# Two-layer graph attention on one core: the projections as seven half-size products, statistics moved ahead, normalization on ScalarE

## The chip, the cores and the metric

One core of a Trainium2 chip runs the whole program. The metric is device time in microseconds, the median of three runs. A core has five engines that run beside each other and wait for one another by semaphores: TensorE (PE, matmuls; its weight loads are shown as PEld), VectorE (DVE), ScalarE (ACT), GpSimd (POOL) and SyncE (SP), which only issues transfers. Each engine takes its own instructions in the order in which the program wrote them.

## What is computed

Two layers over 4096 nodes with 512 features, both with the same 4096 x 4096 matrix `adj`. Cut to what matters:

```python
h = relu(layernorm(x))
q, k, v = h @ Wq.T + bq, h @ Wk.T + bk, h @ Wv.T + bv
x = x + softmax(q @ k.T / sqrt(512) + 2 * adj) @ v          # layer 0
h = relu(layernorm(x))
nX = normalize_per_head(h @ W)                               # 8 heads of 64
att = softmax(where(adj != 0, leaky_relu(at1 + at2.T) * adj, -32768))
x = x + elu(att @ nX + nX)                                   # layer 1
```

## The kernel before, in words

The kernel has three stages, one after the other. The projections (0 to 271 us of the profile) make everything that layer 0 needs of `x`; then comes attention of layer 0, to about 2100 us, in which the features of layer 1 are also made; then attention of layer 1. The change lies in the first stage only.

The projections go by eight blocks (`sb`, 0 to 7) of 512 rows each. A block is four tiles of 128 rows. What is done with a block:

- `load_x` (L531) fetches its rows on SP's queue into `xt`, which has two buffers.
- `normalize` (L537) subtracts the mean and multiplies by the inverse root of the variance. The statistics are `means` (L167; eight DVE instructions, L172 and L173). The root is `inverse_root` (L156): a power on GpSimd (L159), then four small instructions (L161 to L164) on the engine that the caller names, here DVE. Then DVE normalizes the four tiles (L543).
- `hidden` (L548) turns the rows on PE (16 transposes, L553) into `pt`, which has two PSUM buffers; ACT applies the relu and writes `hT` (L554). GpSimd makes four sums and differences of half-size parts of `hT`, called `hS` (L562 to L565). Both are stored, for attention needs them again: it computes the scores by seven half-size products in the form of Strassen's algorithm.
- `values_of` (L570) multiplies `hT` by Wv: 16 matmuls of 128x512 (L574) into `pv`, four PSUM buffers, each read once by DVE, which adds the bias (L578).
- `queries` (L583) multiplies by one matrix A. Since q and k are only used as q times k, Wq and Wk are multiplied once at the start into A (`a_sb`; L648, copied by ACT at L652), and the biases go into the vector `c_sb` (L653). These are again 16 matmuls of 128x512 (L588) into `pq`, the same four PSUM buffers; DVE adds `c_sb`, scales and writes the columns in another order into `qs` (L592). `qs` is stored (L596); GpSimd makes four half-size differences `ts` of it (L605 to L608), stored as well (L610).

The order is written out by hand: `seq` keeps every instruction where the program put it on its engine's queue. After a start, in which the weights are loaded and A is made, round `sb` (1 to 7) is: normalize block sb+1, load block sb+2, values of sb, hidden of sb+1, queries of sb. Some work for layer 1 is slipped in ahead of `queries`: in round 2 `center_weights` (three DVE instructions, L230 to L232), in rounds 3 to 6 `weigh_weights` (L234), which twice lets GpSimd multiply (L237) and DVE sum the product (L238).

At the start come, in this order: block 0 normalized and turned; Wq and Wk transposed on DVE as they land (L464); values of block 0; block 1 normalized; `attention_vectors` (L192; small DVE work for layer 1 and four transfers on ACT's queue); A; `c_sb`; hidden of block 1; queries of block 0.

Lines of later stages that are used below as measures: L719 is a 128x256 matmul of attention in layer 0, L727 the DVE add that reads such a result from PSUM; L258 to L262 are the mean and root of layer 1's normalization, on GpSimd, and L268 is its normalization on ACT.

Of the kernel before, what the change touches and what calls it, by code (L numbers as in the profile page):

```python
# [10 lines left out]
F32 = mybir.dt.float32  # L11
BF16 = mybir.dt.bfloat16
AF = mybir.ActivationFunctionType
ALU = mybir.AluOpType
# [4 lines left out]
P = 128  # L19
# [59 lines left out]
def fast_path(  # L79
# [29 lines left out]
    def sources_of_rows(t):  # L109

        return t.rearrange("p (q c r) -> p c q r", c=SB, r=R)
# [336 lines left out]
    with tc.tile_pool(name="early", bufs=2) as early, tc.tile_pool(name="kv", bufs=1) as kv:  # L448
# [14 lines left out]
        def turn_blocks(t, raw, c):  # L463
            seq(nc.vector.transpose(t.rearrange("p (m r) -> p m r", r=R), raw[:, :, ts(c, R)]))  # L464
# [53 lines left out]
        with tc.tile_pool(name="proj_c", bufs=1) as pc, tc.tile_pool(  # L518
# [10 lines left out]
            bv_sb = early.tile([P, D], F32, name="bv_sb", tag="qt", bufs=16)  # L529

            def load_x(sb):  # L531
                xt = early.tile([P, SB, D], F32, name="xt", tag="ag", bufs=2)
# [1 line left out]
                    seq(nc.sync.dma_start(out=xt[:, b, :], in_=x[ts(sb * SB + b, P), :]))  # L534
                return xt

            def normalize(xt):  # L537
                mv = means(work, [xt[:, b, :] for b in range(SB)], "h")
                var = work.tile([P, SB], F32, name="hv", tag="hv", bufs=1)
                seq(nc.vector.tensor_scalar_add(var, mv[:, :, 1], LN_EPS))  # L540
                rstd = inverse_root(nc.vector, work, var, SB, "h")
                for b in range(SB):
                    seq(nc.vector.tensor_scalar(  # L543
                        xt[:, b, :], xt[:, b, :], mv[:, b, 0:1], rstd[:, b : b + 1],
                        ALU.subtract, ALU.mult,
                    ))

            def hidden(sb, xt):  # L548
                h, sums = hidden_tiles(sb)
                for k in range(KC):  # L550
                    pt = psum.tile([P, 512], F32, name="pt", tag="pt", bufs=2)
                    for b in range(SB):
                        seq(nc.tensor.transpose(pt[:, ts(b, P)], xt[:, b, ts(k, P)], ident))  # L553
                    seq(nc.scalar.activation(  # L554
                        rows_of_sources(h[:, k, :]),
                        pt.rearrange("p (q c r) -> p q c r", c=SB, r=R), AF.Relu,
                    ))
# [4 lines left out]
                seq(nc.gpsimd.tensor_add(sums[:, 0], a["21"], a["22"]))  # L562
                seq(nc.gpsimd.tensor_sub(sums[:, 1], sums[:, 0], a["11"]))
                seq(nc.gpsimd.tensor_sub(sums[:, 2], a["11"], a["21"]))
                seq(nc.gpsimd.tensor_sub(sums[:, 3], a["12"], sums[:, 1]))  # L565
                for t, ap in ((h, h_d), (sums, s_d)):
                    flat = "p a b -> p (a b)" if ap is h_d else "p a b c d -> p (a b c d)"
                    seq(nc.sync.dma_start(out=ap[sb].rearrange(flat), in_=t.rearrange(flat)))

            def values_of(sb):  # L570
                for b in range(SB):
                    pv = psum.tile([P, 512], F32, name="pv", tag="mm", bufs=4)
                    for k in range(KC):
                        seq(nc.tensor.matmul(  # L574
                            pv, hidden_of[sb][0][:, k, ts(b, P)], wv_sb[k],
                            start=k == 0, stop=k == KC - 1,
                        ))
                    seq(nc.vector.tensor_add(v[:, sb * SB + b, :], pv, bv_sb))  # L578


            half_scale = 0.5 / math.sqrt(D)

            def queries(sb):  # L583
                qs = pc.tile([P, KC, GC], F32, name="qs", tag="qs", bufs=1)
                for o in range(KC):
                    pq = psum.tile([P, 512], F32, name="pq", tag="mm", bufs=4)
                    for k in range(KC):
                        seq(nc.tensor.matmul(  # L588
                            pq, a_sb[:, k, ts(o, P)], hidden_of[sb][0][:, k, :],
                            start=k == 0, stop=k == KC - 1,  # L590
                        ))
                    seq(nc.vector.tensor_scalar(  # L592
                        sources_of_rows(qs[:, o, :]), pq.rearrange("p (c q r) -> p c q r", c=SB, r=R),
                        c_sb[:, o : o + 1], half_scale, ALU.add, ALU.mult,
                    ))
# [33 lines left out]
            load_blocks(raw["k"], wkT)  # L629
            xts[1] = load_x(1)  # L630
            seq(nc.sync.dma_start(out=wk_rows, in_=wkT.rearrange("(k p) o -> p k o", p=P)))
            normalize(xts[0])
            hidden(0, xts.pop(0))
            seq(nc.scalar.dma_start(out=bv_sb, in_=bv[None, :].to_broadcast([P, D])))
            seq(nc.scalar.dma_start(out=bq_sb, in_=bq[None, :].to_broadcast([P, D])))
            for name in ("q", "k"):
                for c in range(SB):
                    turn_blocks(turned[name][:, c, :], raw[name], c)
            values_of(0)
            normalize(xts[1])  # L640
            attention_vectors(v[:, 15, :])
            seq(nc.gpsimd.tensor_mul(
                wk_rows, wk_rows, bq_sb.unsqueeze(1).to_broadcast([P, KC, D])
            ))
            for k in range(KC):
                pa_ps = psum.tile([P, 512], F32, name="pa", tag="mm", bufs=4)
                for c in range(SB):
                    seq(nc.tensor.matmul(  # L648
                        pa_ps, turned["q"][:, c, ts(k, P)], turned["k"][:, c, :],
                        start=c == 0, stop=c == SB - 1,  # L650
                    ))
                seq(nc.scalar.copy(a_sb[:, k, :], pa_ps))  # L652
            seq(nc.vector.tensor_reduce(c_sb, wk_rows, AX.X, ALU.add))  # L653
            xts[2] = load_x(2)
            hidden(1, xts[1])
            queries(0)
            for sb in range(1, NS):
                if sb + 1 < NS:
                    normalize(xts[sb + 1])
                if sb + 2 < NS:  # L660
                    xts[sb + 2] = load_x(sb + 2)
                if sb == 1:
                    seq(nc.sync.dma_start(
                        out=w1_sb.rearrange("p k h e -> p k (h e)"),
                        in_=w1.rearrange("(k p) o -> p k o", p=P),
                    ))
                if sb == NS - 2:
                    load_chunk(0, nc.sync)
                    load_adj0(0)
                    load_adj0(SB)  # L670
                if sb == NS - 1:
                    load_hidden(0)
                values_of(sb)
                if sb + 1 < NS:
                    hidden(sb + 1, xts[sb + 1])
                if sb == 2:
                    center_weights()
                elif 3 <= sb < 3 + KC:
# [897 lines left out]
```

## Time and profile before

| | |
|---|---|
| median of three runs | 3968.43 us (3968.31 to 3969.87) |
| the profiled execution | 3965.98 us |
| its span in the profile | 3964.2 us |
| granted clock, mean over the span | 0.991 |
| PE busy | 3774.4 us (95%) |
| end of block 0's queries | 63.39 us |
| a round (63.39 to 93.27) | 29.88 us |
| end of block 7's queries, about | 270.1 us |

One execution was recorded with every instruction's start and end on its engine. A line of the timeline gives the start, the duration, the engine, the line of the kernel, what it writes and reads and in what shape, how many instructions were merged (x4), and in brackets how long the engine had been idle and what released it. The end of a matmul is modelled, so the distance of starts tells more on PE than durations. A matmul of 32-bit floats appears as two records.

### The profile page before, as it was taken

To read this page: it belongs to the slowest core of one execution; us is meant where nothing else is said; L and a number is where in the kernel's file an instruction comes from. 1 tells how busy PE (TensorE), PEld (TensorE's weight loads), DVE (VectorE), ACT (ScalarE), POOL (GpSimd) and SP (SyncE) were. 2 spreads that over 40 slices of the span, in tenths; PEclk is the share of its full clock that TensorE was granted. 3 is DMA by queue.
4 is the path that set the end of the run, shared out by engine and by line. 5 is a ranking of instruction groups with operands and counts; after the bars stand their busy time and mean duration, and the time that the engine had idled before them with its cause. 6 is when DMAs were issued, how large, how long until landed. Compare 5 with 4: busy or idle time off the path is not lost. (4 is left out here: it accounts for less than half of the span.)

```text
span 3964.2 us, 43905 instructions
## 1 busy us (share of the span) xinstructions
PE 3774.4 (95%) x15217; PEld 1789.4 (45%) x15370; DVE 2890.3 (73%) x4328; ACT 1797.0 (45%) x1581; POOL 2564.4 (65%) x1281
## 2 busy tenths in 40 slices
PE   8989999999999999999998899999999999999997
PEld 4446666666666666666653222222222222222222
DVE  5435556565565656556556799999999999999996
ACT  1001011111111111111115688888888888888887
POOL 3432225243242525234256999999999999999998
PEclk9999999999999999999998999999999999999999
DMA  6466656667675766757556544444444444444442
GB/s 208 175 206 193 201 179 204 200 194 211 184 220 161 222 182 191 214 186 222 166 153 189 145 138 146 146 142 142 134 143 144 139 145 146 146 140 146 132 150 79
DMA packets 554407, 670.37 MB, mean 169 GB/s; under 512 B 79808, under 2 KB 397504, under 8 KB 534720
## 3 DMA queue, kind: packets, MB, share of 16 engines
q1 hardware_dynamic: 552112, 665.70, 54.7%
q8 instruction: 122, 2.00, 0.2%
q10 hardware_dynamic: 2064, 1.77, 0.2%
q14 instruction: 109, 0.89, 0.1%
HBM read 495.12 MB, written 172.23 MB: 168 GB/s over the span
## 5 line engine op out<-in xcount | busy, mean ns | idle before, releaser
L985 POOL TENSOR_TENSOR t<-t,g 128x1536 f32<-128x1536 f32 (+1 forms) x512 | 1724.0, 3440 | 47.6 <-DVE t L978 26.9
L1001 PE MATMUL acc<-t,nX 128*64 128x512 f32 x4096 | 996.3, 607 | 72.1 <-ACT t L988 58.0
L737 POOL TENSOR_TENSOR total<-total,aT 128x512 f32<-128x512 f32 x248 | 340.5, 1373 | 1059.0 <-ACT aT L732 1051.9
L988 ACT ACTIVATE t<-t 128x2048 f32<-128x2048 f32 x512 | 975.8, 1906 | 87.7 <-POOL t L985 86.6
L747 PE MATMUL acc<-v,aT 128*128 128x512 f32 x2048 | 961.9, 593 | 0.0
L732 ACT ACTIVATE aT<-aT 128x512 f32<-128x512 f32 x256 | 161.3, 630 | 1323.2 <-DVE aT L727 1315.2
L962 ACT ACTIVATE t<-d 128x1024 f32<-128x1024 f32 x512 | 524.8, 1025 | 239.1 <-PE d L955 216.6
L978 DVE TENSOR_TENSOR t<-t,d 128x1024 f32<-128x1024 f32 x512 | 620.2, 1211 | 7.3 <-ACT t L962 7.3
L955 PE MATMUL d<-nb,ident_b 128*128 128x512 bf16 x1895 | 514.8, 385 | 14.9 <-issue 9.3
L1001 PEld LDWEIGHTS acc<-t,nX 128*64 128x64 f32 x4096 | 250.5, 136 | 597.6 <-issue 340.9
L747 PEld LDWEIGHTS acc<-v,aT 128*128 128x128 f32 x2048 | 389.9, 190 | 272.3 <-issue 244.8
L972 DVE SCALAR_TENSOR_TENSOR d<-u,at2m,d 128x512 f32<-128x512 f32 x542 | 407.3, 752 | 51.9 <-PE d L955 31.1
L727 DVE TENSOR_TENSOR aT<-aT,X 128x256 f32<-128x256 f32 x512 | 215.0, 420 | 279.6 <-PE X L719 276.3
L972 DVE SCALAR_TENSOR_TENSOR t<-u,at2m,d 128x512 f32<-128x512 f32 x482 | 360.0, 747 | 50.0 <-DVE d L972 0.9
L727 DVE TENSOR_TENSOR aT<-aT,Z 128x256 f32<-128x256 f32 x384 | 159.6, 416 | 290.5 <-PE Z L719 285.8
L977 DVE TENSOR_TENSOR t<-d,g 128x512 f32<-128x512 f32 (+1 forms) x512 | 366.3, 715 | 4.3 <-DMA g<-gT_d 1.4
L950 PE MATMUL d<-z,z 6*128 6x512 bf16 x2048 | 252.2, 386 | 45.5 <-DVE t L977 22.7
L711 DVE SCALAR_TENSOR_TENSOR gs<-ng,aT 128x512 f32<-128x512 bf16 x256 | 286.0, 1117 | 10.3 <-DMA gT_d<-gs 1.7
L950 PEld LDWEIGHTS <-z 6*128 6x128 bf16 x2048 | 76.8, 91 | 456.0 <-issue 451.9
L719 PE MATMUL Z<-qt,hS 128*128 128x256 f32 x1024 | 266.0, 383 | 8.6 <-DVE aT L727 8.4
L955 PEld LDWEIGHTS <-ident_b 128*128 128x128 bf16 x2048 | 159.2, 98 | 242.9 <-issue 123.4
L719 PE MATMUL X<-qt,hS 128*128 128x256 f32 x1024 | 263.9, 381 | 0.0
(161 smaller groups left out, 3120.6 us busy)
## 6 DMA issues: line engine op xcount, KB each, us to landing
g<-gT_d SPq DMA_DIRECT2D x128, 1024.0 KB, 5.5
ag<-in_adj_dram SPq DMA_DIRECT2D x256, 256.0 KB, 5.2
hT<-h_d SPq DMA_DIRECT2D x64, 1024.0 KB, 5.9
hS<-s_d SPq DMA_DIRECT2D x64, 1024.0 KB, 8.2
gT_d<-gs SPq DMA_DIRECT2D x256, 256.0 KB, 2.7
nb<-nT_d SPq DMA_DIRECT2D x128, 512.0 KB, 5.3
nT_d<-ng SPq DMA_DIRECT2D x256, 128.0 KB, 3.1
z<-z_d SPq DMA_DIRECT2D x143, 128.0 KB, 4.7
```

The lines of the kernel that those rows point to most:

```text
L719: seq(nc.tensor.matmul(out, a, b, start=start and k == 0, stop=k == 1, skip_group_check=not start,))
L727: seq(nc.vector.tensor_add(p, p, part))
L737: seq(nc.gpsimd.tensor_add(totals[ic], totals[ic], p))
L747: seq(nc.tensor.matmul(sums[ic][b], probs[s][:, ts(b, P)], v[:, jt, :], start=jt == 0, stop=jt == NB - 1))
L955: seq(nc.tensor.matmul(pair[hh // 2][:, hh % 2, :], ident_b, ng[:, jt % JB, :], start=False, stop=True))
L962: seq(nc.scalar.activation(t[:, 0:2, :], zs[n][0], AF.Relu, scale=4.0))
L972: seq(nc.vector.scalar_tensor_tensor(pair[1][:, e, :] if e > 1 - mine else t[:, 2, :], u4[:, e, :], at2m[:, jt, h : h + 1], pair[1][:, e, ...
L977: seq(nc.vector.tensor_mul(t[:, HG - mine : HG, :], pair[1][:, 2 - mine : 2, :], g))
L978: seq(nc.vector.tensor_add(t[:, 0:2, :], t[:, 0:2, :], pair[0]))
L985: seq(nc.gpsimd.tensor_mul(t[:, 0:mine, :], t[:, 0:mine, :], g))
L988: seq(nc.scalar.activation(logits[n], logits[n], AF.Exp))
L1001: seq(nc.tensor.matmul(grp["acc"][hf][ts(e, HD), :], nX[jt // SB][:, jt % SB, hg * HG + 2 * hf + e, :], t[:, 2 * hf + e, :], start=jt == 0 ...
```

## The change

What it does:

- Each projection of a block (values and queries) is computed by seven products of half-size parts instead of eight. The parts are 256 rows x 256 columns, in two *lanes* of 128. `seven` goes through the products in four steps, lane 0 then lane 1 in each: (2, 1), (5, 6), (3, 7), (4). A PSUM tile `X` and one `Z` of 128x256 stand for each lane, two buffers of each in all; products accumulate in them, and after each product DVE adds the tile's present content to a quarter of the result (`take`): 14 DVE instructions of 128x256 for a projection. Sums of the hidden rows are at hand in `hS`; sums of Wv (`sum_wv`) and of A (`sum_a`) are made once on GpSimd.
- The scale that L592 applied goes into A and `c_sb`.
- The statistics of a block stand two rounds ahead: `deviations_of` block sb+2 stands between `hidden` of sb+1 and `queries` of sb. The small instructions of the root, and two more that make a shift of mean times root, are on GpSimd. The normalization of the four tiles is done by ACT, after `queries` of sb in the program.
- The PSUM tile `pa` has two buffers instead of four; `bv_sb` lies in another pool.

The diff, cut to its core:

```diff
-            def normalize(xt):
+            def deviations_of(xt):
                 mv = means(work, [xt[:, b, :] for b in range(SB)], "h")
                 var = work.tile([P, SB], F32, name="hv", tag="hv", bufs=1)
-                seq(nc.vector.tensor_scalar_add(var, mv[:, :, 1], LN_EPS))
-                rstd = inverse_root(nc.vector, work, var, SB, "h")
+                seq(nc.gpsimd.tensor_scalar_add(var, mv[:, :, 1], LN_EPS))
+                rstd = inverse_root(nc.gpsimd, work, var, SB, "h")
+                shift = work.tile([P, SB], F32, name="hs", tag="hs", bufs=2)
+                seq(nc.gpsimd.tensor_mul(shift, mv[:, :, 0], rstd))
+                seq(nc.gpsimd.tensor_scalar_mul(shift, shift, -1.0))
+                return rstd, shift
+
+            def normalize(xt, rstd, shift):
                 for b in range(SB):
-                    seq(nc.vector.tensor_scalar(
-                        xt[:, b, :], xt[:, b, :], mv[:, b, 0:1], rstd[:, b : b + 1],
-                        ALU.subtract, ALU.mult,
+                    seq(nc.scalar.activation(
+                        xt[:, b, :], xt[:, b, :], AF.Identity,
+                        scale=rstd[:, b : b + 1], bias=shift[:, b : b + 1],
                     ))
...
+            def seven(product, take):
+                x, z = [
+                    [psum.tile([P, H], F32, name=name, tag=name, bufs=2) for _ in range(2)]
+                    for name in ("X", "Z")
+                ]
+                for n, todo in enumerate((
+                    ((2, z, "11", True), (1, x, "11", False)), ((5, z, "22", True), (6, x, "12", True)),
+                    ((3, z, "12", False), (7, x, "22", False)), ((4, x, "21", True),),
+                )):
+                    for lane in range(2):
+                        for which, t, _, _ in todo:
+                            product(lane, which, t[lane], which in (1, 2, 5))
+                        for _, t, block, first in todo:
+                            take(lane, block, t[lane], first)
...
             def values_of(sb):
-                for b in range(SB):
-                    pv = psum.tile([P, 512], F32, name="pv", tag="mm", bufs=4)
...
-                    seq(nc.vector.tensor_add(v[:, sb * SB + b, :], pv, bv_sb))
+                def take(pair, block, part, first):
+                    half = ts(int(block[1]) - 1, H)
+                    to = v[:, sb * SB + 2 * pair + int(block[0]) - 1, half]
+                    seq(nc.vector.tensor_add(to, part, bv_sb[:, half] if first else to))
...
             def queries(sb):
...
-                    seq(nc.vector.tensor_scalar(
-                        sources_of_rows(qs[:, o, :]), pq.rearrange("p (c q r) -> p c q r", c=SB, r=R),
-                        c_sb[:, o : o + 1], half_scale, ALU.add, ALU.mult,
-                    ))
+                    if first:
+                        seq(nc.vector.tensor_scalar_add(to, part, c_sb[:, o : o + 1]))
+                    else:
+                        seq(nc.vector.tensor_add(to, part, to))
...
-            normalize(xts[0])
+            normalize(xts[0], *deviations_of(xts[0]))
             hidden(0, xts.pop(0))
+            sum_wv()
...
             for name in ("q", "k"):
                 for c in range(SB):
                     turn_blocks(turned[name][:, c, :], raw[name], c)
+            of_next = deviations_of(xts[1])
             values_of(0)
-            normalize(xts[1])
+            normalize(xts[1], *of_next)
             attention_vectors(v[:, 15, :])
...
-                pa_ps = psum.tile([P, 512], F32, name="pa", tag="mm", bufs=4)
+                pa_ps = psum.tile([P, 512], F32, name="pa", tag="mm", bufs=2)
...
-                seq(nc.scalar.copy(a_sb[:, k, :], pa_ps))
+                seq(nc.scalar.mul(a_sb[:, k, :], pa_ps, half_scale))
             seq(nc.vector.tensor_reduce(c_sb, wk_rows, AX.X, ALU.add))
+            seq(nc.vector.tensor_scalar_mul(c_sb, c_sb, half_scale))
+            sum_a()
             xts[2] = load_x(2)
             hidden(1, xts[1])
+            of_next = deviations_of(xts[2])
             queries(0)
+            normalize(xts[2], *of_next)
             for sb in range(1, NS):
-                if sb + 1 < NS:
-                    normalize(xts[sb + 1])
...
                 values_of(sb)
                 if sb + 1 < NS:
                     hidden(sb + 1, xts[sb + 1])
+                if sb + 2 < NS:
+                    of_next = deviations_of(xts[sb + 2])
                 if sb == 2:
                     center_weights()
                 elif 3 <= sb < 3 + KC:
                     weigh_weights(sb - 3)
                 queries(sb)
+                if sb + 2 < NS:
+                    normalize(xts[sb + 2], *of_next)
```

More of the change, by code (lines that the diff above doesn't have):

```diff
@@ L528, in fast_path @@
             c_sb = pc.tile([P, KC], F32, name="c_sb")
-            bv_sb = early.tile([P, D], F32, name="bv_sb", tag="qt", bufs=16)
+            bv_sb = pc.tile([P, D], F32, name="bv_sb")
+            wv_sums, a_sums = [
+                [early.tile([P, KC // 2, H], F32, name=name, tag="qt", bufs=16) for _ in range(4)]
+                for name in ("wvs", "as")
+            ]
             def load_x(sb):
@@ L568, in hidden @@
                     seq(nc.sync.dma_start(out=ap[sb].rearrange(flat), in_=t.rearrange(flat)))
-            def values_of(sb):
-                for b in range(SB):
-                    pv = psum.tile([P, 512], F32, name="pv", tag="mm", bufs=4)
[L573 to L576, printed above, removed]
-                        ))
-                    seq(nc.vector.tensor_add(v[:, sb * SB + b, :], pv, bv_sb))
@@ L581, in fast_path @@
-            half_scale = 0.5 / math.sqrt(D)
+            def seven(product, take):
+                x, z = [
+                    [psum.tile([P, H], F32, name=name, tag=name, bufs=2) for _ in range(2)]
+                    for name in ("X", "Z")
+                ]
+                for n, todo in enumerate((
[7 more added lines that the diff above has]
+                            take(lane, block, t[lane], first)
@@ new lines, in pair_product, with wv_side @@
+            def pair_product(out, a, b, start):
+                for k in range(2):
+                    seq(nc.tensor.matmul(
+                        out, a[k], b[k], start=start and k == 0, stop=k == 1,
+                        skip_group_check=not start,
+                    ))
+            SIDES = {1: ("A11", "B11"), 2: ("A12", "B21"), 3: ("S4", "B22"), 4: ("A22", "T4"),
+                     5: ("S1", "T1"), 6: ("S2", "T2"), 7: ("S3", "T3")}
+            def wv_side(name):
+                if name[0] == "T":
+                    return [wv_sums[int(name[1]) - 1][:, k, :] for k in range(2)]
+                k0, half = 2 * (int(name[1]) - 1), int(name[2]) - 1
+                return [wv_sb[k0 + k][:, ts(half, H)] for k in range(2)]
@@ new lines, in sum_wv @@
+            def sum_wv():
+                b = {f"{k + 1}{i + 1}": wv_side(f"B{k + 1}{i + 1}") for i in range(2) for k in range(2)}
+                t = [[wv_sums[e][:, k, :] for k in range(2)] for e in range(4)]
+                for out, left, right in (
+                    (t[0], b["12"], b["11"]), (t[1], b["22"], t[0]), (t[2], b["22"], b["12"]),
+                    (t[3], b["21"], t[1]),
+                ):
+                    for k in range(2):
+                        seq(nc.gpsimd.tensor_sub(out[k], left[k], right[k]))
@@ new lines, in values_of, with product @@
+            def values_of(sb):
+                def product(pair, which, out, start):
+                    a, b = SIDES[which]
+                    pair_product(out, side_a(sb, pair, a), wv_side(b), start)
+                def take(pair, block, part, first):
+                    half = ts(int(block[1]) - 1, H)
+                    to = v[:, sb * SB + 2 * pair + int(block[0]) - 1, half]
+                    seq(nc.vector.tensor_add(to, part, bv_sb[:, half] if first else to))
+                seven(product, take)
@@ new lines, in fast_path, with a_side, sum_a @@
+            half_scale = 0.5 / math.sqrt(D)
+            def a_side(name, o):
+                if name[0] == "S":
+                    return [a_sums[int(name[1]) - 1][:, k, ts(o, P)] for k in range(2)]
+                k0, half = 2 * (int(name[2]) - 1), int(name[1]) - 1
+                return [a_sb[:, k0 + k, half * H + o * P : half * H + (o + 1) * P] for k in range(2)]
+            def sum_a():
+                a = {f"{i + 1}{k + 1}": a_sb[:, 2 * k : 2 * k + 2, ts(i, H)]
+                     for i in range(2) for k in range(2)}
+                seq(nc.gpsimd.tensor_sub(a_sums[0], a["22"], a["21"]))
+                seq(nc.gpsimd.tensor_add(a_sums[1], a_sums[0], a["11"]))
+                seq(nc.gpsimd.tensor_sub(a_sums[2], a["21"], a["11"]))
+                seq(nc.gpsimd.tensor_sub(a_sums[3], a["12"], a_sums[1]))
@@ L583, in queries, with rows_side, product, take @@
+            def rows_side(sb, name):
+                h, sums = hidden_of[sb]
+                if name[0] == "T":
+                    return [sums[:, (2, 1, 0, 3)[int(name[1]) - 1], k] for k in range(2)]
+                h = h.rearrange("p k (t j r) -> p k j t r", j=2, r=P)
+                return [h[:, 2 * (int(name[1]) - 1) + k, int(name[2]) - 1] for k in range(2)]
             def queries(sb):
                 qs = pc.tile([P, KC, GC], F32, name="qs", tag="qs", bufs=1)
[L585 to L592, printed above, removed]
-                        sources_of_rows(qs[:, o, :]), pq.rearrange("p (c q r) -> p c q r", c=SB, r=R),
-                        c_sb[:, o : o + 1], half_scale, ALU.add, ALU.mult,
-                    ))
+                def product(o, which, out, start):
+                    a, b = SIDES[which]
+                    pair_product(
+                        out.rearrange("p (t r) -> p t r", r=P), a_side(a, o), rows_side(sb, b), start
+                    )
+                def take(o, block, part, first):
+                    o = 2 * (int(block[0]) - 1) + o
+                    to = qs[:, o, :].rearrange("p (q t j r) -> p j t q r", q=SB, j=2, r=R)
+                    to = to[:, int(block[1]) - 1]
+                    part = part.rearrange("p (t q r) -> p t q r", q=SB, r=R)
+                    if first:
+                        seq(nc.vector.tensor_scalar_add(to, part, c_sb[:, o : o + 1]))
+                    else:
+                        seq(nc.vector.tensor_add(to, part, to))
+                seven(product, take)
```

## The prediction

> **What bounds the kernel now.** First the page's engine shares, then busy time by stage, to see who sets the pace where the change is.
>
> ```profile
> PE 3774.4 (95%) x15217; PEld 1789.4 (45%) x15370; DVE 2890.3 (73%) x4328; ACT 1797.0 (45%) x1581; POOL 2564.4 (65%) x1281
> ```
>
> ```profile
> 0.00:63.40 63.40, 49.56 (x129) 23.70 (x130) 38.12 (x78) 8.09 (x13) 18.48 (x18) 0.97 0.64 200
> 63.40:271.00 207.60, 204.55 (x545) 95.06 (x543) 88.00 (x170) 13.04 (x24) 82.54 (x66) 1.00 0.56 192
> 271.00:2100.00 1829.00, 1793.33 (x6181) 1142.58 (x6183) 1069.29 (x1922) 236.06 (x379) 646.69 (x619) 0.99 0.65 195
> ```
>
> Columns: stretch, its length, busy us of PE, PEld, DVE, ACT, POOL, granted clock, DMA share, GB/s. The change touches only 0 to 271 us, the projections. From 63.4 on PE is busy 98.5% of that stage: fewer matmul columns are worth their full time there, so long as nobody makes PE wait. So I read the timeline of one round (row block 5) for who releases whom.
>
> ```profile
> 196.63 1.04 PE L553 MATMUL pt<-ident,xt 128*128 128x128 f32 x8
> ...
> 199.04 13.90 PE L588 MATMUL pq<-hT,a_sb 128*128 128x512 f32 x32
> 199.87 0.33 SPq L568 DMA_DIRECT2D h_d<-hT  x1
> 199.92 1.27 POOL L562 TENSOR_TENSOR hS<-hT 128x512 f32<-128x512 f32 x1 [11.09 <-ACT hT L554]
> ...
> 204.93 2.49 POOL L237 TENSOR_TENSOR prod<-w_sb,a_sb 128x512 f32<-128x512 f32 x2
> 205.00 0.33 SPq L568 DMA_DIRECT2D s_d<-hS  x1
> 206.23 0.69 DVE L238 TENSOR_REDUCE w1a_sb<-prod 128x8 f32<-128x512 f32 x1 [8.70 <-POOL prod L237]
> 207.45 0.69 DVE L238 TENSOR_REDUCE w1a_sb<-prod 128x8 f32<-128x512 f32 x1 [0.54 <-POOL prod L237]
> 208.05 2.25 DVE L592 TENSOR_SCALAR qs<-pq,c_sb 128x512 f32<-128x512 f32 x3
> ```
>
> Call V the moment the value products end (196.63). Queries start at V+2.41. DVE stands for 8.70 us at L238, for GpSimd, and reads the first query result only at V+11.42, three at once: PE had finished those long before. It did not stop because `pq` has four PSUM buffers (3.43 us of matmuls each): 13.7 us of cover. That cover is what I watch.
>
> Last, what a stopped PE costs when it restarts (280 us, the start of attention):
>
> ```profile
> 273.20:279.50 6.30, 0.00 (x0) 0.00 (x0) 3.96 (x8) 0.00 (x0) 1.71 (x2) 0.90 0.95 323
> 279.50:282.00 2.50, 2.48 (x6) 2.04 (x7) 0.79 (x2) 0.00 (x0) 0.00 (x0) 0.50 0.95 263
> 282.00:284.50 2.50, 2.50 (x8) 1.96 (x7) 0.47 (x2) 0.00 (x0) 0.00 (x0) 0.50 0.72 268
> 284.50:287.00 2.50, 1.99 (x9) 1.39 (x8) 0.84 (x2) 0.63 (x1) 0.61 (x1) 0.89 0.01 3
> ```
>
> After 6.3 us of rest, half clock for about 5 us: some 2.6 us lost. After 31.8 us (2.8 us of rest) passes stand 0.85 us apart instead of 0.43 until 35.6: 1.8 us lost.
>
> [...] L232 took 3.35 us and held L563 to 3.20, while L578 (one PSUM input) kept 0.69 beside L608.
>
> **The change part by part.**
>
> *Seven products.* The trace has two records (passes) per f32 matmul. 128x512 passes stand 0.429 us apart: 32 for a projection of a block, 13.73 us. 128x256, as attention has them already:
>
> ```profile
> 602.97 1.03 PE L719 MATMUL Z<-qt,hT 128*128 128x256 f32 x4
> ...
> 603.83 1.03 PE L719 MATMUL X<-qt,hT 128*128 128x256 f32 x4
> ```
>
> Four passes 0.86 us apart, 0.2145 each, weight loads hidden (0.19). Now 7 products x 2 lanes x 4 passes = 56: 12.01 us. Gain 1.72 us a projection, 3.44 a round.
>
> *Results read in pieces.* 14 DVE adds of 128x256 instead of 4 of 512. L727 takes 0.42; permuted ones, half of L592's 0.75, 0.38 to 0.75 if halving saved nothing; I take 0.42. A round: 28 x 0.42 + 3.3 of statistics = 15.1 of 26.4 us. Throughput costs nothing. But the buffers do: X and Z have two each, one per lane. After products 2 and 1 of both lanes (4 x 0.858 = 3.43 us) product 5 must wait until DVE has read lane 0's Z: cover falls from 13.7 to 3.43 us. PE stops at V+2.41+3.43 = V+5.84 unless that read has ended.
>
> *What stands on DVE ahead of that read.* After the last value read (V+0.62) the statistics of block sb+2, moved here: four L172/L173 pairs, 3.3 us as at 183.77 to 187.09, to V+3.9. Round 1: the read then follows at once; no stop. Round 2: L230 2.28, L231 0.2, L232 2.1 after waiting for a GpSimd sum: to V+9.5. Read 0.42, signal 0.05: PE resumes at V+9.97, 4.1 late. Rounds 3 to 6 have the two L238, which wait for GpSimd, and there the eight small root instructions now stand between the sums (to V+8.30) and L237. The same eight of layer 1 (L258, L159, L161 to L164, L261, L262) run 512.01 to 515.69, 3.7 us; one L161 is stretched there, so 3.3 to 3.7: I take 3.5. Rounds 3 to 5: V+11.42+3.5+0.47 = V+15.39, 9.55 late. Round 6 has no roots: V+11.89, 6.05 late. Together 4.1 + 28.65 + 6.05 = 38.8 us. Each restart is at half clock: [...] the two above give 1.8 and 2.6; 2.2 x 5 = 11. Sum 49.8.
>
> *Start.* Roots on GpSimd and four ACT passes (0.80 each, L268) instead of DVE's bring the first transposes some 2 us later. That doesn't count: DVE's queue has the K transposes (DMA, 28.68 to 31.17), then block 1's statistics (3.31, to 34.5), and only then the first read of block 0's values. Before, four buffers held all values and PE was through at 29.06. Now it stops after four products and resumes at 34.95; 10 products 8.58, half clock 2.2: 45.7. A's product 13.73 (warm now): 59.5; hidden 2.33; queries 12.01: 73.8, against 63.39. Plus 10.4. (The weight sums, 8 x 0.65 on GpSimd, end near 29, before 34.95. A's sums follow its last copy, the first ready 1.5 us after, wanted 5.8 us after. The attention vectors' DMAs wait on ACT's queue behind block 1's normalization, to 41, and land by 50; DVE's 8 to 10.6 us on them, 2.5 for c_sb and 3.3 of statistics end by 63, when the first query result appears, with 2.4 us to spare.)
>
> *Rounds.* 1 to 6: -3.44 each; block 7's two projections -3.44: -24.1.
>
> *At nothing.* DVE's normalization (1.91) and roots leave a queue with room. ACT's four come after the relus, 22 us before they are wanted; they would cost if GpSimd's roots ended after V+23. The x loads keep their place on SP behind the t stores and land about 11.7 us after the queries' end; statistics want the first at 12.6; SP gets no new transfer. The scaling moved into ACT's copy and c_sb: one DVE instruction of 0.17. GpSimd's sums come before any use. End: last read 0.42 instead of 0.75: -0.3; then the 4.28 us for q_d as before.
>
> Sum: 10.4 - 24.1 + 49.8 - 0.3 = +35.8 us. On the profiled execution, 3965.98: 4001.8; on the median, 3968.43, 2.45 above it: 4004.
>
> **The rivals.** *The products pay.* If the reads come in time, PE stays the bound: 10.4 - 24.1 - 0.3 = -14, 3954. The point is one place: the first query read must end by V+5.84. For it: the 98.5%, and round 1 is such a round. Against it: L238's own 8.70 us wait, measured, ends at V+11.42 even without the roots. *Roots beside other work, no half clock:* waits 4.1 + 4 x 6.05 = 28.3, nothing for the clock at either place: 8.2 - 24.1 + 28.3 - 0.3 = +12, 3981. *DVE becomes the bound:* needs over 0.82 us a read; even 0.75 leaves 24.3 of 26.4. *The seven products save nothing:* a pass at 0.245 us or more would do it, giving 4028; 603.83 says 0.2145.
>
> **How the numbers follow.** Stops as worked out, 0.85: 3991 without any half-clock loss, 4010 with 2.8 each and slow reads; own range 3988 to 4011. Products pay, 0.07; near balance, stops half as long and the start partly hidden, 0.04 (3968, some 8 either way); GpSimd hidden, 3981, 0.02; dearer passes or DVE-bound, 0.02. The range 3985 to 4012 leaves out the sign change and the dear passes. A measurement here tells about 0.2% from no change. Faster 0.07, same 0.04, slower 0.89.
>
> **What would show it.** Right: projection matmuls at 0.86 us a product; PE idle 9 to 10 us once in each of rounds 3 to 5, 6 in round 6, 4 in round 2, none in round 1, released by DVE's first query read, after L238; a granted clock of about 0.5 after each; an idle PE up to 35 us; queries of block 0 ending near 74 and attention starting near 306. Wrong: if PE runs on through rounds 3 to 6, the order on DVE's queue doesn't do what I say, and 3954 is the case. If the stops are there and shorter, GpSimd's roots cost less than 3.5.

## The result, and the profile after

| | before | changed |
|---|---|---|
| median | 3969.15 us (3968.31 to 3970.69, 4 runs) | 3998.04 us (3996.67 to 3999.42, 4 runs) |
| profiled execution | 3965.98 us | 3999.06 us |
| its span | 3964.2 us | 3997.3 us |
| granted clock over the span | 0.991 | 0.985 |

The changed kernel is 28.9 us slower: ratio 1.0076, interval 1.0064 to 1.0088. The two profiled executions differ by 33.1 us. That is no contradiction: the one of before lies 3.17 us under its median, the one of the changed kernel 1.02 us over. I compare the traces with each other.

The page's engine line and busy time by stage of the changed kernel (columns as in the prediction):

```profile
PE 3775.8 (94%) x15754; PEld 1868.9 (47%) x15754; DVE 2913.9 (73%) x4417; ACT 1820.6 (46%) x1613; POOL 2585.8 (65%) x1349
```

```profile
0.00:68.98 68.98, 47.24 (x176) 33.57 (x177) 36.10 (x89) 14.24 (x22) 33.33 (x52) 0.93 0.62 184
68.98:300.27 231.29, 191.74 (x878) 165.04 (x877) 112.28 (x246) 30.35 (x48) 89.67 (x101) 0.90 0.51 173
300.27:2130.00 1829.73, 1791.90 (x6182) 1141.80 (x6181) 1068.21 (x1921) 234.41 (x378) 644.00 (x615) 0.99 0.65 194
```

The shares of the whole span hardly move; the middle stage tells it. PE was busy 98.5% of 207.6 us and is busy 83% of 231.3 us, at a granted clock of 0.90 instead of 1.00. It has less work there (191.7 us against 204.6, some 10 us of the 191.7 only because the clock was halved, as worked out below) and stands longer. (The middle stretch of the changed kernel as shown ends about 1 us before block 7's queries do.)

The timeline of round 3, where V, the end of the value products, is 141.52 (here and below, lines of a timeline that don't bear on the point are left out):

```profile
144.47 0.66 DVE L172 BATCH_NORM_STATS2 hst<-xt 128x6 f32<-128x512 f32 x1
...
146.38 1.03 PE L599 MATMUL X<-hT,a_sb 128*128 128x256 f32 x4
...
148.45 1.26 POOL L576 TENSOR_TENSOR hS<-hT,hS 128x512 f32<-128x512 f32 x1
149.80 0.23 POOL L545 TENSOR_SCALAR hv<-hmv 128x4 f32<-128x4 f32 x1
...
152.62 0.23 POOL L549 TENSOR_SCALAR hs<-hs 128x4 f32<-128x4 f32 x1
152.82 2.49 POOL L237 TENSOR_TENSOR prod<-w_sb,a_sb 128x512 f32<-128x512 f32 x2
154.12 0.69 DVE L238 TENSOR_REDUCE w1a_sb<-prod 128x8 f32<-128x512 f32 x1 [8.77 <-POOL prod L237]
155.34 0.69 DVE L238 TENSOR_REDUCE w1a_sb<-prod 128x8 f32<-128x512 f32 x1 [0.54 <-POOL prod L237]
155.95 0.47 DVE L679 TENSOR_SCALAR qs<-Z,c_sb 128x256 f32<-128x256 f32 x1
156.48 2.08 PE L599 MATMUL Z<-hS,as 128*128 128x256 f32 x4 [9.06 <-DVE qs L679]
158.34 1.92 PE L599 MATMUL X<-hS,as 128*128 128x256 f32 x4
160.05 1.36 PE L599 MATMUL Z<-hS,as 128*128 128x256 f32 x4
161.25 1.03 PE L599 MATMUL X<-hS,as 128*128 128x256 f32 x4
```

Read it from the bottom. PE ran out of free buffers after its fourth product, at 147.4, and stood 9.06 us for DVE's first read of a query product (L679). The product it reads had begun at 143.79 and is shown as 1.03 us long, but DVE took it only at 155.95: L238 stood ahead of it, 8.77 us idle for GpSimd's product (L237), and L237 stood behind the eight root instructions (149.80 to 152.85), which stood behind GpSimd's sums of the hidden rows (L576 is the last). After the stop the first products are 1.86 and 1.71 us apart instead of 0.86. The granted clock of that stop and of the 4.8 us after it:

```profile
146.00:156.48 10.48, 1.42 (x8) 0.91 (x6) 1.76 (x3) 2.93 (x4) 8.63 (x13) 0.71 0.43 175
156.48:161.30 4.82, 4.82 (x13) 3.94 (x14) 2.21 (x5) 0.00 (x0) 0.00 (x0) 0.56 0.00 0
```

Rounds 1 to 6, from the start of a block's values to the start of the next block's, took:

| round | before | changed | PE stood | rest over 26.45 |
|---|---|---|---|---|
| 1 | 29.88 | 26.45 | 0 | 0 |
| 2 | 29.88 | 34.01 | 4.91 | 2.65 |
| 3 | 29.88 | 37.85 | 9.06 | 2.34 |
| 4 | 29.88 | 37.72 | 9.09 | 2.18 |
| 5 | 29.88 | 37.62 | 9.08 | 2.09 |
| 6 | 29.87 | 34.30 | 5.91 | 1.94 |

The last column is what the rounds took beyond the product time and the stop. In rounds 2 to 6 about 0.17 us of it belongs to the stop: a product is shown as 1.03 us long, but the next one can follow after 0.86, and the stop is counted from the shown end.

Block 0's queries end at 68.98 instead of 63.39, and attention starts at 301.85 instead of 271.13.

### The profile page after: what moved, and what is told of

It is laid out like the page before. It is cut to its first block, busy times and chain, and to the rows that moved or that the text cites. A ratio compares the mean times of both kernels' runs of the same rounds, so it can differ in the third digit from the quotient of the medians.

```text
span 3997.3 us, 45136 instructions
## 1 busy us (share of the span) xinstructions
PE 3775.8 (94%) x15754; PEld 1868.9 (47%) x15754; DVE 2913.9 (73%) x4417; ACT 1820.6 (46%) x1613; POOL 2585.8 (65%) x1349
## 5 line engine op out<-in xcount | busy, mean ns | idle before, releaser
L1051 PE MATMUL d<-nb,ident_b 128*128 128x512 bf16 x2048 | 537.0, 385 | 2.1 <-DMA nb<-nT_d 2.1
```

Of the source, the lines that this page charges most:

```text
L1051: seq(nc.tensor.matmul(pair[hh // 2][:, hh % 2, :], ident_b, ng[:, jt % JB, :], start=False, stop=True))
```

## Experiments

My theory after the result was the prediction's: the seven products are worth what they should be, and the first query read comes too late because L238 and, through GpSimd, the roots stand ahead of it. Rivals: it is the statistics that are in the way; or the roots alone; or the loss is elsewhere than in the stops. The kernel before was measured again beside the experiments: 3969.81 us (9 runs) beside the first four and 3967.0 us (17 runs) beside the last three; the ratios are to these. The changed kernel was not measured again, so differences of medians to its 3998.04 us are uncertain by 2 or 3 us. In the experiments' profiles the line numbers are shifted by up to twenty.

**1. The two DVE sums behind the queries.** `weigh_weights` is split: GpSimd's products stay where they are, the sums go behind `queries(sb)`.

```diff
             seq(nc.gpsimd.tensor_mul(t, w1_sb[:, k], aa[e]))
-            seq(nc.vector.tensor_reduce(w1a_sb[:, k, e, :], t, AX.X, ALU.add))
+            prods[k, e] = t
...
                 queries(sb)
+                if 3 <= sb < 3 + KC:
+                    sum_weights(sb - 3)
```

> Only the two DVE sums of the layer-1 weights (L238) move, from ahead of the query reads of rounds 3 to 6 to behind them; their GpSimd products, the roots and everything else stay. Theory (PE stops because L238 stands on DVE's queue ahead of the first query read, and restarts at half clock): the stops of rounds 3 to 6 vanish, each of these rounds takes 26.4 us as round 1 does, against 37.8, 37.7, 37.6 and 34.3, so about 41.7 us less; round 2 keeps its 34.0. Time near 3956. Rival (the statistics and roots moved ahead are what holds the reads): rounds 3 to 5 stay above 33 us and the time above 3985.

Measured: 3956.09 us (3955.57 to 3962.24), ratio 0.9965, interval 0.9952 to 0.9979. Rounds 3 to 6 took 26.45, 26.44, 26.44 and 26.45 us. The timeline of DVE in round 3 (V = 140.85):

```profile
145.91 0.48 DVE L685 TENSOR_SCALAR qs<-Z,c_sb 128x256 f32<-128x256 f32 x1 [0.32 <-PE Z L605]
...
155.41 0.48 DVE L685 TENSOR_SCALAR qs<-X,c_sb 128x256 f32<-128x256 f32 x1 [0.38 <-PE X L605]
155.81 1.27 DVE L244 TENSOR_REDUCE w1a_sb<-prod 128x8 f32<-128x512 f32 x2
157.00 0.41 DVE L640 TENSOR_TENSOR v<-Z,bv_sb 128x256 f32<-128x256 f32 x1
```

From the third query read on every read of this round waits for PE (0.32 to 0.44 us), and PE for none; the sums stand where nobody waits. The statistics and the roots are still where the change put them, and cost these rounds nothing. Round 2, which has `center_weights` and was left alone, still stood 4.92 us. So the two DVE instructions ahead of the read are the cause in rounds 3 to 6, 41.7 us of trace (147.49 us for the four rounds down to 105.78) and 42 us of median.

**2. The roots behind the products.** L238 stays ahead of the read, but GpSimd does the roots after L237.

```diff
-                    of_next = deviations_of(xts[sb + 2])
+                    mv = stats_of(xts[sb + 2])
...
                     weigh_weights(sb - 3)
+                if sb + 2 < NS:
+                    of_next = roots_of(mv)
                 queries(sb)
```

> Only GpSimd's order changes: the eight root instructions stand behind the products of the layer-1 weights instead of ahead of them. Theory: L238 is released 3.1 us earlier (the roots' length in this trace), so PE's stops in rounds 3 to 5 shrink from 9.1 to about 6.0 us, as in round 6, and the rounds from about 37.7 to 34.5; together 9 to 10 us less, about 3988.5. Rival (the roots run beside other work and cost nothing): no change.

Measured: 3991.0 us (3981.48 to 3993.34), ratio 1.0053, interval 1.004 to 1.0067. The timeline of round 3:

```profile
148.75 0.69 DVE L238 TENSOR_REDUCE w1a_sb<-prod 128x8 f32<-128x512 f32 x1 [0.54 <-POOL prod L237]
149.11 1.04 POOL L159 TENSOR_TENSOR hr<-hv,mhalf 128x4 f32<-128x4 f32 x1
149.36 0.47 DVE L684 TENSOR_SCALAR qs<-Z,c_sb 128x256 f32<-128x256 f32 x1
149.89 2.07 PE L604 MATMUL Z<-hS,as 128*128 128x256 f32 x4 [5.91 <-DVE qs L684]
```

Rounds 3 to 5 stand 5.91 us each, as round 6 does without roots, and last 34.45, 34.29 and 34.22 us: 10.2 us less together. (The medians differ by 7.0; the runs of this kernel lie 12 us apart, and its start and its later stages both moved in the trace, as told below.) The roots were worth about 3.2 us in each of three rounds, and L238 alone still costs a stop and the clock after it. That rules out the roots as the whole cause. It also answers the rival of 3981: here the waits are what that rival supposed, and the kernel is still 10 us slower than its 3981, which had the half clock at nothing.

**3. PE kept busy in the stops.** 5, 10, 10, 10 and 6 extra matmuls of 128x512, whose result nobody reads, after the fourth product of the queries in rounds 2 to 6.

```diff
+                    if n == 0 and fill:
+                        spare = psum.tile([P, 512], F32, name="pa", tag="mm", bufs=2)
+                        for _ in range(fill):
+                            seq(nc.tensor.matmul(spare, a_sb[:, 0, 0:P], a_sb[:, 1, :], start=True, stop=True))
```

> In the stops of rounds 2 to 6 PE is given extra 128x512 matmuls whose result nobody reads: 5, 10, 10, 10 and 6 of 0.858 us each, a little less than each stop (4.9, 9.1, 9.1, 9.1, 5.9). The result of the kernel is unchanged. Theory (a stop costs its own length and then 1.9 to 2.7 us at half clock): the reads come when they came, PE restarts at full clock, each of the five rounds ends 1.9 to 2.7 us earlier, together about 11.6; about 3986.5. Rival (the slow matmuls after a stop come from the reads or from something else than the rest): no gain, or the extra matmuls are added to the time.

Measured: 3990.58 us (3987.02 to 3998.49), ratio 1.0057, interval 1.0043 to 1.007. The timeline of round 3:

```profile
146.46 8.75 PE L599 MATMUL pa<-a_sb 128*128 128x512 f32 x20
155.20 0.48 DVE L685 TENSOR_SCALAR qs<-Z,c_sb 128x256 f32<-128x256 f32 x1
155.73 1.13 PE L605 MATMUL Z<-hS,as 128*128 128x256 f32 x4 [0.52 <-DVE qs L685]
156.69 1.03 PE L605 MATMUL X<-hS,as 128*128 128x256 f32 x4
```

The next product follows after 0.96 us instead of 1.86. Rounds 2 to 6 took 31.63, 35.82, 35.83, 35.82 and 32.65 us, 9.8 less together than in the changed kernel, with the read as late as there (PE goes on at V+15.00; it was V+14.96). In each of the five rounds the first product after the stop took 0.96 or 0.97 us and the next 0.86 or 0.87. PE did more work and the program ended earlier: those 9.8 us were the clock. In round 3, 9.37 us over 26.45 remain, little more than the lateness of the read alone (9.06). Block 0 happened to end 1.6 us later in this execution, so attention started 8.2 us earlier; the medians differ by 7.5, with runs of this kernel 11 us apart.

**4. The start: block 1's statistics behind the value reads.** Also the attention vectors' loads from ACT's queue to SP's, so that they don't stand behind the normalization on ACT.

```diff
+            attention_loads(nc.sync)
...
-            of_next = deviations_of(xts[1])
             values_of(0)
+            of_next = deviations_of(xts[1])
             normalize(xts[1], *of_next)
```

> Only the start changes: block 1's statistics stand on DVE behind the reads of block 0's values instead of ahead, and the four loads of the attention vectors go on SP's queue behind the rows of Wk, so that they don't wait for block 1's normalization. Theory: PE resumes block 0's values when the K transposes end (23.6 us) instead of at 29.9, and block 0's queries end near 63.3 instead of 68.98: 5 to 6 us less, about 3992.5. Rival (another wait is next: the weight sums on GpSimd, or c_sb and block 2's statistics ahead of the first query read): block 0's queries end later than 66.

Measured: 4000.54 us (3997.7 to 4001.24), ratio 1.0074, interval 1.0061 to 1.0088. A miss: no gain. The timeline says why:

```profile
35.76 7.03 PE L741 MATMUL pa<-v 128*128 128x512 f32 x16
39.68 0.31 POOL L547 TENSOR_SCALAR hv<-hmv 128x4 f32<-128x4 f32 x1 [11.81 <-DVE hmv L173]
...
44.51 2.93 ACT L556 ACTIVATE xt<-xt,hs,hr 128x512 f32<-128x512 f32 x4 [27.27 <-POOL hs L551]
47.34 1.06 ACT L745 ACTIVATE a_sb<-pa 128x512 f32<-128x512 f32 x2
```

The values did end earlier: PE stands 3.61 us there instead of 8.57 and begins A at 35.76 instead of 40.84. But A has only two buffers now, which ACT empties (L745), and ACT's queue has the normalization of block 1 ahead of those copies. Its roots, moved back with the statistics, end near 44.5. PE stood 5.18 us in the middle of A, and block 0's queries ended at 72.27 instead of 68.98. The wait was not removed; it moved from DVE's queue to ACT's, and cost more. The move had changed when three engines worked, and I had looked at one.

**5. The seven products alone.** Statistics, roots and normalization as before, on DVE at the head of the next round.

```diff
-            normalize(xts[1], *of_next)
+            normalize(xts[1])
...
             for sb in range(1, NS):
+                if sb + 1 < NS:
+                    normalize(xts[sb + 1])
```

> The seven products alone: statistics, roots and normalization stay on DVE one round ahead, at the head of the round, as in the kernel before. Theory (what stands on DVE ahead of the first read stops PE): now the values stop too, in rounds 1 to 6, because 7.8 us of normalization stand ahead of their reads against a cover of 3.43 us: 5.4 us and about 2.2 at half clock each; the queries of rounds 3 to 6 stop 6.0 and 2 us each, as no roots stand ahead of the products. Together near 79 us of stops against 49 in the changed kernel; with a start some 6 us later, near 4033. Rival (moving the statistics is what stops PE): faster than 3998.

Measured: 4048.89 us (4044.32 to 4049.36), ratio 1.0203, interval 1.0187 to 1.0218. The timeline of round 3 shows a second stop, at the values:

```profile
159.41 1.92 DVE L548 TENSOR_SCALAR xt<-xt,hmv,hr 128x512 f32<-128x512 f32 x4
161.24 0.42 DVE L628 TENSOR_TENSOR v<-Z,bv_sb 128x256 f32<-128x256 f32 x1
161.80 1.19 PE L593 MATMUL Z<-wvs,hS 128*128 128x256 f32 x2 [5.26 <-DVE v L628]
```

Such a stop of 5.26 us is in each of rounds 1 to 6, for DVE's statistics, roots and normalization ahead of the first value read; rounds 3 to 6 have 5.91 more at the queries. The direction is as expected, the size is not (4033 expected): about half of the 16 us is the start, where block 0 ended at 83.33, with stops of 12.52 and 9.14 us, later than I had allowed for. So the rest of the change is no burden to the seven products but some 50 us of help (4048.9 against 3998.0); it only doesn't go far enough.

**6. The rest alone.** Statistics ahead, roots on GpSimd, normalization on ACT, with the 16 matmuls and four buffers of before: `values_of` and `queries` are those of before again.

> Statistics two rounds ahead, roots on GpSimd and normalization on ACT alone; the projections stay 16 matmuls of 128x512 with four PSUM buffers. Theory: in rounds 3 to 5 the first query read comes at V+14.8 us as in the changed kernel, but four buffers cover to V+16.1, so PE never stops and the rounds stay at 29.88 us; the K transposes come some 7 us earlier, as in the changed kernel, so block 0's queries end near 60.7 instead of 63.4. Time 3966 to 3969. Rival (the moved statistics cost by themselves): rounds longer than 29.9 us, time above 3980.

Measured: 3965.81 us (3962.02 to 3969.29, 13 runs), ratio 0.9997, interval 0.9989 to 1.0006: no difference. Busy time by stage, and round 3 (V = 134.76):

```profile
0.00:61.55 61.55, 48.93 (x128) 23.54 (x129) 28.97 (x68) 16.87 (x25) 23.87 (x40) 1.00 0.70 206
61.55:268.46 206.91, 204.56 (x545) 94.91 (x543) 66.64 (x108) 27.68 (x44) 88.84 (x100) 1.00 0.56 193
```

```profile
137.04 13.90 PE L594 MATMUL pq<-hT,a_sb 128*128 128x512 f32 x32
147.37 0.69 DVE L238 TENSOR_REDUCE w1a_sb<-prod 128x8 f32<-128x512 f32 x1 [8.51 <-POOL prod L237]
149.21 2.72 DVE L598 TENSOR_SCALAR qs<-pq,c_sb 128x512 f32<-128x512 f32 x4
```

PE is busy 98.9% of the rounds (29.74 us each). The same L238, as late, stops nobody here: the first query read (L598) comes at V+14.45, as in the changed kernel (V+14.43), and PE runs its 32 passes through, for four buffers of 3.43 us cover it. DVE has 21 us less to do in the rounds, and each round is 0.14 us shorter; the time of the program shows no gain.

**7. What the first six point to.** The sums behind the value reads of the next round; `center_weights` in four pieces behind the queries of rounds 1 to 4; block 1's statistics behind the values, its normalization between the second and third of A's copies on ACT; the attention loads on SP.

```diff
+                if k == 1:
+                    normalize(xts[1], *of_next)
...
                 values_of(sb)
+                if 4 <= sb < 4 + KC:
+                    sum_weights(sb - 4)
...
-                if sb == 2:
-                    center_weights()
-                elif 3 <= sb < 3 + KC:
+                if 3 <= sb < 3 + KC:
                     weigh_weights(sb - 3)
                 queries(sb)
+                if sb <= KC:
+                    center_weights(sb - 1)
```

> The changed kernel with nothing long on DVE ahead of a first read: the sums of the layer-1 weights stand behind the value reads of the next round, the centring of these weights goes in four pieces behind the queries of rounds 1 to 4, block 1's statistics stand behind block 0's value reads, block 1's normalization between the second and third copy of A on ACT, and the attention vectors' loads on SP. Theory: no stop in any round, 26.4 us each; A is not held up, block 0's queries end near 64; attention starts near 247 instead of 302, and 271 before. Time near 3946, 0.6% below the kernel before. Rival (the early statistics or GpSimd become the next wait): one or more rounds above 28 us.

Measured: 3948.91 us (3948.19 to 3950.32), ratio 0.9954, interval 0.9941 to 0.9968: faster than both kernels. Busy time by stage, up to the start of attention:

```profile
0.00:65.33 65.33, 47.48 (x176) 33.51 (x177) 38.84 (x89) 15.65 (x24) 35.98 (x52) 0.97 0.66 194
65.33:252.76 187.43, 182.45 (x882) 158.36 (x880) 117.45 (x257) 28.82 (x46) 88.84 (x100) 1.00 0.62 213
```

DVE is busier than in either kernel (117 us of 187) and stops PE in the rounds for 0.72 us at most: they take 26.45, 27.40, 27.41, 27.40, 27.41 and 26.44 us, the extra 0.96 where a piece of `center_weights` stands ahead of a value read. With the centring out of the way round 2 has lost its stop too. Attention starts 18.4 us earlier than before; the medians differ by 18.1. At the start PE still stands 3.62 and 1.29 us, so it gives back 1.9 us against before (65.33 and 63.39). Expected were 64 for that end and 247 for the start of attention, which came at 252.8: the four longer rounds are 3.8 us of it, the start 1.3.

## Why the prediction was right, step by step

| term, profiled executions | predicted | measured |
|---|---|---|
| start, to the end of block 0's queries | +10.4 | +5.6 |
| seven products, rounds 1 to 7 (7 x 3.43) | -24.1 | -24.0 |
| PE stands, rounds 2 to 6 | 38.8 | 38.05 |
| half clock after it | 11 | 11.2 |
| end | -0.3 | -0.3 |
| attention and what follows | 0 | +2.4 |
| sum | +35.8 | +33.1 |

The measured terms up to attention add up to 30.6; attention starts 30.7 us later. The start was forecast 4.8 us too long, and the 2.4 us of attention, for which I have no cause, hide half of that in the sum: so much of the closeness is luck. The medians differ by 28.9 us, 6.9 less than forecast; 4.2 of these come from where the two profiled executions lie about their medians.

**Seven products**: right. A product takes 0.86 us and round 1, which has no stop, 26.45 us, 3.43 less than 29.88. Experiment 1 shows four more such rounds (3 to 6) with the products untouched.

**Cover of two buffers a tile**: right. PE stopped in round 3 at V+5.9 (forecast V+5.84). That cover is what makes L238 matter is seen from both sides: with four buffers of 3.43 us L238 stops nobody (experiment 6), with two a tile it does unless it is moved (experiment 1). Experiment 6 differs in the form of the products too; the seven products with more buffers were not run.

**The first query read**: right in place and order, somewhat less in size. GpSimd reached the roots at V+8.28 (V+8.30), but they took 3.05 us where I took 3.5, so PE resumed at V+14.96 instead of V+15.39. In round 2 it went the other way, 4.91 for 4.1: L231 took 0.99 us there where I had 0.2, and L232, at its 3.30, ended at V+10.3 where I had V+9.5 (V = 107.51). These misses partly cancel.

**Half clock**: 1.94 to 2.65 us a stop, 2.2 predicted. Experiment 3 shows that it is the clock and not the read. By the granted clock in the trace of the changed kernel (0.50 until then, 1.00 behind it) the full clock was back 4.86, 4.24, 3.92, 3.75 and 3.43 us after PE went on, in rounds 2 to 6. (In round 3 two products took 1.86 and 1.71 us, the third 1.20.) Half of these times, 10.1 us together, is what the half clock cost; with five times 0.17 us that belongs to the stops it makes up nearly all of the 11.2.

**Start**: the mis-sized term, 4.8 of the 10.4. The step was "DVE's queue has the K transposes (DMA, 28.68 to 31.17), then block 1's statistics". That time was copied from the trace of before without asking what the transfer itself had waited for. In the changed kernel (start, timeline) the transfers are issued at 9.64, not from 15.19 on:

```profile
9.64 4.57 SPq L458 DMA_DIRECT2D v<-in_wkT_dram  x4
21.12 2.49 DVE L464 STREAM_TRANSPOSE v<-v 128x512 f32<-128x512 f32 x4 [2.74 <-DMA v<-in_wkT_dram]
...
28.52 0.69 DVE L172 BATCH_NORM_STATS2 hst<-xt 128x6 f32<-128x512 f32 x1 [1.83 <-DMA xt<-in_x_dram]
29.35 0.39 DVE L634 TENSOR_TENSOR v<-Z,bv_sb 128x256 f32<-128x256 f32 x1
29.89 2.05 PE L599 MATMUL Z<-wvs,hS 128*128 128x256 f32 x4 [8.57 <-POOL hv L545]
```

(The releaser that the last line names came last by the profile; the read at 29.35 is the one that frees the buffer.) The statistics then ran beside their own loads, waited 0.49 and 1.83 us for them, and PE resumed at 29.89 instead of 34.95. The rest of the start was as worked out, 5 us earlier throughout. SP's waits in the first 40 us of before show what I had not looked at:

```profile
SPq L458 <- DMA v<-in_wqT_dram: 4.8, 1, 4.8
SPq L458 <- DMA bv_sb<-in_bv_dram: 3.9, 1, 3.9
...
SPq L458 <- DMA a_sb<-in_a1T_dram: 1.1, 1, 1.1
```

SP held the first of the four loads of Wk (L458) for one of its own, the third load of Wq, which landed at 15.17, and only the other three for small loads of ACT's queue. (`a_sb<-in_a1T` is one of the attention vectors, not A.) In the changed kernel the waits for `bv_sb` and `a_sb` at L458 are gone, and the 6.8 us for `bv_sb` fall on loads of `x` instead:

```profile
SPq L539 <- DMA bv_sb<-in_bv_dram: 6.8, 1, 6.8
...
SPq L458 <- DMA wv_sb<-in_wvT_dram: 3.2, 3, 1.7
```

Which part of the change did this, experiments 5 and 6 tell: with the seven products alone the last four loads are issued from 14.4 on and the second set of transposes starts at 28.86, as before; with ACT's normalization and no seven products, from 9.7 on, as in the changed kernel. It goes with the work put on ACT's queue ahead of those small loads: ACT's queue issued six of them from 15.31 to 17.67 in the kernel before; in the changed kernel it issued two, at 17.39 and 17.82, and the four of the attention vectors behind block 1's normalization, from 32.89 on. In the kernel before Wk's four loads were issued at 15.19, 19.44, 20.11 and 21.56, each within 0.02 us of the landing of a load that SP's waits name: the third of Wq, `bv_sb`, the bias of q and the first attention vector (15.17, 19.42, 20.09 and 21.55). In the changed kernel they went out at 9.64, 11.15, 12.04 and 13.30, and SP's waits at L458 name no load of ACT's queue. Why a load on one queue was held for one on another, and what decides for which, was not shown; that stays open.

The start is also the least steady part: with the same code there block 0's queries ended at 68.98 in the changed kernel and at 68.27, 65.8 and 70.56 in experiments 1, 2 and 3, following the landing of block 1's last tile (28.50, and 27.72, 25.81 and 29.42 in those three).

**Attention and what follows**: its code is the same and it took 2.4 us longer. Over the seven experiments that stretch varies by more than that (3691.7 us in experiment 2, 3701.0 in experiment 1), so I give it no cause.

**The rivals.** That the products pay was a question of one place, and experiment 1 makes it come true by moving two instructions: 3956.09, the 3954 of that rival within 2 us. That it is so close is in part chance: round 2 still lost 7.6 us, and the start cost 5.5 us less than the 10.4 which that rival had. DVE as the bound: no, it works 112 us of 231, and more in experiment 7.

## What to carry to other kernels

Smaller products with fewer buffers can shorten the work and still lose: work out for how long the buffers cover a late reader (here 13.7 us fell to 3.4), and look for whatever stands on the reader's queue ahead of its first read, above all an instruction that itself waits for a third engine. Such an instruction is free as long as the cover holds and costs its full lateness, plus a slow restart (here 1.94 to 2.65 us), once it doesn't; here moving it behind the reads was the remedy, and making it 3.2 us earlier (experiment 2) was not enough. Before a time is copied from the old trace into a forecast, ask what that event had waited for, and whether the change moves that; and when a wait is taken off one queue, walk through the other queues that the moved work now stands on.

## What the runs showed of the hardware that I had not expected

- Unread matmuls in a stop made the program faster: 41 of them in five stops saved 9.8 us of trace (experiment 3).
- The restart after 4.9 us of rest cost no less than after 9.1 us (2.65 and 2.09 to 2.34 us). The granted clock stood at 0.50 for 6.82 us about the stops of rounds 2 and 6 and for 10.24 us about those of 3 to 5; 3.43 to 4.86 us of that came after PE went on, the most in round 2, after the shortest stop, and the loss is about half of that part. What sets these lengths was not shown.
- Two rests of the same length were followed by different things. In experiment 7 PE stood 1.96 us before 273.61, in attention; its second product then took 1.41 us instead of 0.86 and the four passes of 128x512 behind it 2.86 instead of 1.72. After a rest of 1.96 us before 292.99 in the kernel before they took 0.86 and 1.72.
- Work on ACT's queue went with a move of SP's transfers: the first load of Wk was issued at 9.64 instead of 15.19 us, the last at 13.30 instead of 21.56. The traces show what SP waited for in each case, not why.
- Some small instructions took longer where they ran beside one of the other engine of the pair DVE and GpSimd. L231 (128x32) took 0.99 us beside GpSimd's L575, which ended 0.04 us before it, and 0.18 in the kernel before. GpSimd's L545 took 2.15 us beside L232 and 0.23 in round 3. In experiment 4 the eight root instructions took 4.8 us (39.68 to 44.47) instead of 3.05, beside DVE's 128x512 work on the attention vectors (0.40 to 0.69 us each). Which instructions lengthen each other was not isolated.
